# Mixing matrices of four quarters per product, contexts and mixed bias by batch, and an accumulating bias transfer in a four-layer kernel

## The chip, the cores and the metric

The kernel runs on one core of one Trainium2 chip. The core has five engines that work side by side: TensorE (PE, matmuls, with its weight loads shown as PEld), VectorE (DVE), ScalarE (ACT), GpSimd (POOL) and SyncE (SP). Here SP issues nearly all DMA transfers and POOL the rest; each of the two works through its own queue in order, and a transfer that waits for something holds up what is behind it in its queue. The metric is the time of one execution in microseconds (us) on the device. The time before is 2033.86 us, the median of three runs (2033.33 to 2036.02).

## The reference, cut to what matters

The input `x` is 32 batches of 64 rows by 1024 columns, in float32. Four layers follow one another, each of the form `x = x + ffn(cond(x))`, where `cond` mixes rows under a condition vector of 128 values per batch.

```python
# layers 0 and 3: every batch has its own 64 x 64 mixing matrix and bias
h = gelu(embedding @ W0 + b0); h = gelu(h @ W1 + b1)
att = softmax(h @ W2 + b2)                             # 32 x 8
agg_w = einsum('bk,koi->boi', att, weight[..., 0])     # 8 matrices of 64 x 64, mixed
agg_b = att @ bias_k                                   # "mixed bias", 32 x 64
out = einsum('boi,bih->boh', agg_w, x) + agg_b[:, :, None]
# layers 1 and 2: a grouped convolution over the columns
out = conv(x, weight) + (c @ c_weight.T)[:, :, None] + bias[None, :, None]   # "context"
# ffn of layer 0: top-1 routing over 8 low-rank experts
# ffn of layer 1: row-wise int8 quantization, a 1024 x 1024 product, + bias[None, :]
# ffn of layer 2: dense product + bias, and top-2 routing over 16 experts
# ffn of layer 3: squared-relu and latent products, then a layer norm
```

## The kernel before, in words

The 2048 rows are 16 tiles of 128 rows, so a tile `j` holds two batches. A tile of `x` is kept in a padded form of 8 segments of 129 columns (`W` = 1032), which makes the convolution's windows plain slices. Between the layers the tiles lie in DRAM as `xd[1]`, `xd[2]` and `xd[3]`. The program is written as straight Python loops; a planner orders the instructions of each engine and each queue by its own costs and by when buffers come free, so loads appear earlier in the SP queue than in the text.

**Start.** `condition(0)` and `attention(0, ...)` (lines 135 to 166) make `att[0]`, the attention transposed, 8 by 32. `aggregate` (lines 168 to 184) mixes the matrices: for each of four quarters `q` it loads 8 rows by 1024 values of `wk` (L174), makes two products of 32 rows by 512 (L178; each is two records in the trace), evicts one on ACT (L180) and one on DVE (L182), and stores 32 by 1024 values to DRAM (L183). `block_diagonal` (L192) loads these as `aw`, 128 by 128 per tile.

**Layer 0** (lines 399 to 434) is a software pipeline over `j`: `project` (L311, `z`), `route` (L320 with the mixed bias `bb`, L321 with `aw`), `turn`, `give` (L351 to L353, which stores `xd[1][j]` and loads it back by rows with L233 as `g`), and `conv1` (L242, L245), which adds the context `cb1`. `contexts` (lines 199 to 215) makes `cb` for all 128 partitions at once: POOL multiplies the weights by the condition for 8 batches at a time (L206, `cpr`), a product with a matrix of ones sums over the partitions (L213), and DVE adds `fside` (L214); it does so four times. For layer 1 its temporaries come from the six-buffer pool of `xT` and `w1` (`w4`). At `j` = 8 and 9 the condition of layer 3 is computed.

**Layer 1** (lines 439 to 586) begins when `cmax` of all tiles is known. In every step PE makes two products of `y` split in two parts (`hi`, `lo`, L509) and small ones for the row scales (L467, L483, `rb`), DVE does most of the quantization, and `deliver` (lines 514 to 517) multiplies on DVE into one of two buffers `t` (L516) and adds to `x` on POOL (L517). The tile then goes to `xd[2]` (L580). `x` is loaded up to five tiles ahead (`x_from`, L121), into a buffer that the store of an older tile frees, and POOL adds the bias to it (L555), in two halves. At `j` = 8, `contexts(2, ...)` makes layer 2's context.

**Layer 2** (lines 589 to 747) starts with the rows of two tiles and one convolution. Then come `aggregate(3, ...)` and, at lines 726 to 737, the mixed bias of layer 3 for all partitions, `ab3`: POOL (L729), a product with ones (L736) and a copy on ACT (L737), four times. After these the convolution of tile 1 and the steady loop follow: a logits product (L612, `lg`), 32 records of the base product (L654), transposes, 32 records of the experts' product (L664). Beside it, pieces of layer 3's weights are loaded (L686), summed on DVE and stored (`usum`, `dsum`, L695). `ab3` and layer 3's `aw` are first read in `mix` (L794, L795).

**Layer 3** (lines 750 to 1032) works in four blocks of four tiles. `second` makes seven products by the scheme of a fast matrix multiplication; `times` (lines 926 to 939) streams five weight tiles and uses each for two tiles `t`. After the last, "3", DVE adds (L775), takes statistics (L954) and `leave` normalizes (L960 to L965) and stores (L966).

Of the kernel before, what the change touches and what calls it, by code (L numbers as in the profile page):

```python
# [39 lines left out]
P = 128  # L40
# [22 lines left out]
def four_layers(ctx: ExitStack, tc: tile.TileContext, a: dict, out: bass.AP):  # L63
# [32 lines left out]
    hp = const("hp", a["hp"], (NB, P + NT + 2 * KC), nc.sync)  # L96
# [53 lines left out]
    def attention(n, h2, W2):  # L150
# [11 lines left out]
        ps = bank(f"attT_{n}", (KC, NB))  # L162
        nc.tensor.transpose(ps, ex, ident[:NB, :NB])
        atT = cst.tile([KC, NB], F32, name=f"attT_{n}")
        nc.vector.tensor_copy(atT, ps)
        return atT

    def aggregate(n, tmp_in, tmp_out):

        d = dram.tile([NB, 64, 64], F32, name=f"agg_{n}")  # L170
        flat = d.rearrange("b i o -> b (i o)")
        for q in range(4):
            w = tmp_in(f"wk_{n}_{q}")[:KC, :]
            nc.sync.dma_start(out=w, in_=a[f"wk_{n}"][:, ts(q, D)])  # L174
            t = tmp_out(f"ag_{n}_{q}")[:NB, :]
            for h in range(2):
                ps = bank(f"ag_{n}_{q}_{h}", (NB, HF))
                nc.tensor.matmul(ps, att[n], w[:, ts(h, HF)], start=True, stop=True)  # L178
                if h == 0:
                    nc.scalar.copy(t[:, ts(h, HF)], ps)  # L180
                else:
                    nc.vector.tensor_copy(t[:, ts(h, HF)], ps)  # L182
            nc.sync.dma_start(out=flat[:, ts(q, D)], in_=t)  # L183
        return d
# [14 lines left out]
    def contexts(n, pool, tmp):  # L199

        cw = small.tile([P, 64], F32, tag="ctxw", name=f"ctxw{n}")
        nc.gpsimd.dma_start(out=cw, in_=a[f"cwT_{n}"])
        cb = pool.tile([P, NB, 64], F32, name=f"cb{n}")
        for q in range(4):
            pr = tmp(f"cpr{n}_{q}").rearrange("p (b o) -> p b o", o=64)[:, 0:8, :]
            nc.gpsimd.tensor_tensor(  # L206
                pr,
                cw[:, None, :].to_broadcast([P, 8, 64]),
                condT[:, ts(q, 8), None].to_broadcast([P, 8, 64]),
                ALU.mult,  # L210
            )
            ps = bank(f"cb{n}_{q}", (P, 8, 64))
            nc.tensor.matmul(ps, ones, pr, start=True, stop=True)  # L213
            nc.vector.tensor_tensor(cb[:, ts(q, 8), :], ps, fside[:, None, :].to_broadcast([P, 8, 64]), ALU.add)  # L214
        return cb

    def mixed_bias(n, j, bk, eng):
# [4 lines left out]
            att[n][:, ts(j, 2), None].to_broadcast([KC, 2, 64]),  # L222
# [36 lines left out]
    with tc.tile_pool(name="q", bufs=1) as qp:  # L259
# [15 lines left out]
        with tc.tile_pool(name="l0", bufs=1) as lp:  # L275
# [15 lines left out]

            load(0)
# [107 lines left out]
            for j in range(NT + 6):  # L400
# [20 lines left out]
                if j == 1:  # L421
                    cb1 = contexts(1, lp, w4)
# [16 lines left out]
        with tc.tile_pool(name="w1", bufs=2) as wp:  # L439
            bias1 = small.tile([P, D], F32, tag="bias1", bufs=1, name="bias1")  # L440
            nc.gpsimd.dma_start(out=bias1, in_=a["bias1"].partition_broadcast(P))
# [95 lines left out]
            for j in range(-3, NT):  # L537
# [12 lines left out]
                if j == 8:  # L550
                    cb2 = contexts(2, k2, lambda name: wp.tile([P, HF], F32, tag="t", name=name))
                if 0 <= j + 2 < NT:
                    xs[j + 2] = x_from(f"x1_{j + 2}", xd[1][j + 2])
                    for h in range(2):
                        nc.gpsimd.tensor_tensor(  # L555
                            xh(xs[j + 2], h), xh(xs[j + 2], h), halved(bias1[:, ts(h, HF)]), ALU.add
                        )
# [32 lines left out]
    with tc.tile_pool(name="l2", bufs=1) as lp, tc.tile_pool(name="w2", bufs=7) as wp, tc.tile_pool(  # L590
# [134 lines left out]

        ab3 = c3.tile([P, NT, P], F32, name="ab3")
        for q in range(4):
            bb = w4(f"bb3_{q}")[:KC, 0:HF].rearrange("k (b o) -> k b o", o=64)
            nc.gpsimd.tensor_tensor(  # L729
                bb,  # L730
                att[3][:, ts(q, 8), None].to_broadcast([KC, 8, 64]),
                bk3[:, None, :].to_broadcast([KC, 8, 64]),
                ALU.mult,
            )
            ps = bank(f"ab3_{q}")
            nc.tensor.matmul(ps, ones[:KC, :], bb.rearrange("k b o -> k (b o)"), start=True, stop=True)  # L736
            nc.scalar.copy(ab3[:, ts(q, 4), :].rearrange("p j t -> p (j t)"), ps)  # L737
# [13 lines left out]
    with ExitStack() as l3:  # L751
# [158 lines left out]
        def second(k, between):  # L910
# [15 lines left out]
            def times(name, ps, lhs, src, go):  # L926
                for q in range(NP3 // 2):
                    w = stream(f"d_{b}_{name}_{q}", src(q))
                    for n in range(2):
                        for t in range(2):  # L930
                            i = 2 * q + n
                            nc.tensor.matmul(  # L932
                                ps[t],
                                lhs(i)[:, ts(t, P)],
                                w[:, ts(n, HF)],
                                start=(go and i == 0),
                                stop=(i == NP3 - 1),
                                skip_group_check=not go,
                            )
# [16 lines left out]
            def leave(t):  # L956
                for i in range(2):
# [45 lines left out]
            for o, p in zip(c(0, 1), p3):  # L1003
                add(o, p, o)
            finish(0, 1)
            leave(0)
# [127 lines left out]
```

## Time and profile before

| what | value |
|---|---|
| median of three runs | 2033.86 us (2033.33 to 2036.02) |
| the profiled execution's own time | 2033.69 us |
| its span, first to last instruction | 2031.9 us |
| PE busy | 1939.8 us, 95% of the span |
| DVE busy | 772.2 us, 38% |
| ACT busy | 241.8 us, 12% |
| POOL busy | 218.8 us, 11% |
| DMA moved | 316.50 MB, 156 GB/s in the mean |
| mean granted TensorE clock | 0.976 |

A group line of the profile gives the source line, the engine, the operation, the tile that is written and those that are read, shapes, how often it occurs, and behind a bar the busy time, the mean of one, and the idle time before it with what ended it. In the timeline a line is start, duration, engine, line, operation; the brackets hold the engine's idle time before it and what it waited for. In the list of waits a line has the waiter, what it waited for, and then the total in us, the number of waits and the longest. The granted clock is the share of full speed that TensorE was allowed. Matmul ends are modelled, so PE's busy time says where it was occupied rather than how well.

### The profile page before, as it was taken

Reading aid. Unit: us, or ns where it says so; the run is one execution under the profiler, and the core shown is the slowest. Engines: PE = TensorE matmul, PEld = TensorE weight load, DVE = VectorE, ACT = ScalarE, POOL = GpSimd, SP = SyncE. Lnnn points to the kernel's source line nnn. Section 1 sums busy time; section 2 is a strip of 40 time slices with the busy share of each in tenths; the row PEclk is TensorE's granted clock in tenths of the full one; section 3 lists DMA queues with packets and bytes.
Section 4 is the critical chain, followed back from the end, with each engine's and each line's share of the span. In section 5 each row is a group of like instructions: output and inputs, shape, how many; then the busy total and the mean of one; then the engine's idle time right before and its main releaser. Section 6 shows DMA issues by size and latency. Waiting matters only on the chain.

```text
span 2031.9 us, 18897 instructions
## 1 busy us (share of the span) xinstructions
PE 1939.8 (95%) x7338; PEld 1230.3 (61%) x7338; DVE 772.2 (38%) x1566; ACT 241.8 (12%) x611; POOL 218.8 (11%) x181
## 2 busy tenths in 40 slices
PE   6999897899999999999699999999999999999997
PEld 3777475645555555554488544885448864488643
DVE  3655596545541212121444224441234422353213
ACT  1221685310000000000000000000000000000000
POOL 2002055610000000000200001100001000010000
PEclk9989898979999999999799999999999999999999
DMA  7856353587950101001544544644445454454542
GB/s 229 301 189 219 112 186 132 182 255 265 320 177 32 63 32 63 11 21 43 197 156 145 167 144 166 207 157 165 145 172 196 159 167 155 155 187 147 171 150 91
DMA packets 134393, 316.50 MB, mean 156 GB/s; under 512 B 17424, under 2 KB 51248, under 8 KB 134304
## 3 DMA queue, kind: packets, MB, share of 16 engines
q1 hardware_dynamic: 133568, 313.09, 45.4%
q0 software_dynamic: 736, 2.21, 0.3%
q8 instruction: 58, 0.95, 0.2%
q14 instruction: 31, 0.25, 0.0%
HBM read 257.39 MB, written 57.87 MB: 155 GB/s over the span
## 4 chain that ended last, share of the span: by engine, by line
PE 87%; DMA 5%; DVE 3%; issue 2%; POOL 2%; ACT 1%; SPq 0%; POOLq 0%; DVEq 0%; ACTq 0%
PE d L932 24%; PE u L842 23%; PE o L664 11%; PE o L654 10%; PE conv L242 5%; PE oo L509 2%; DMA xd<-x 2%; PE z L311 2%; PE mix L794 2%; PE o L351 1%; PE lg L612 1%; PE g L525 1%; DMA x<-xd 1%; DMA wk<-in_wk_dram 1%; PE gp L801 1%
## 5 line engine op out<-in xcount | busy, mean ns | idle before, releaser
L932 PE MATMUL d<-d,h 128*128 128x512 f32 x640 | 278.8, 593 | 0.0
L664 PE MATMUL o<-bt,pT 128*128 128x512 f32 x512 | 224.0, 595 | 0.5 <-ACT pT L661 0.3
L654 PE MATMUL o<-base,yT 128*128 128x512 f32 x512 | 223.0, 593 | 0.0
L932 PE MATMUL d<-d,s 128*128 128x512 f32 x480 | 208.3, 593 | 0.0
L932 PEld LDWEIGHTS d<-d,h 128*128 128x128 f32 x640 | 120.3, 190 | 144.6 <-issue 140.9
L775 DVE TENSOR_TENSOR h<-u,h 128x256 f32<-128x256 f32 x200 | 84.8, 424 | 263.0 <-PE u L842 261.6
L664 PEld LDWEIGHTS o<-bt,pT 128*128 128x128 f32 x512 | 96.0, 190 | 118.3 <-issue 114.6
L654 PEld LDWEIGHTS o<-base,yT 128*128 128x128 f32 x512 | 96.1, 190 | 114.8 <-issue 111.0
L932 PEld LDWEIGHTS d<-d,s 128*128 128x128 f32 x480 | 90.7, 190 | 114.5 <-issue 113.3
L923 POOL TENSOR_TENSOR fin<-xf,beta 128x512 f32<-128x512 f32 x32 | 53.1, 1687 | 982.6 <-DMA out_dram<-fin 955.7
L842 PE MATMUL u<-y,uc 128*128 128x256 f32 x640 | 151.4, 379 | 0.9 <-DVE h L775 0.9
L842 PE MATMUL u<-y,ua 128*128 128x256 f32 x640 | 151.6, 379 | 0.0
L842 PE MATMUL u<-t,ub 128*128 128x256 f32 x640 | 146.9, 383 | 0.0
L242 PEld LDWEIGHTS conv<-cw,g 128*128 128x128 f32 x1024 | 123.9, 197 | 19.6 <-issue 16.6
L842 PEld LDWEIGHTS u<-t,ub 128*128 128x128 f32 x640 | 123.0, 192 | 16.9
L666 DVE TENSOR_TENSOR x<-x,o 128x512 f32<-128x512 f32 x32 | 21.9, 687 | 291.9 <-PE o L664 291.9
L842 PEld LDWEIGHTS u<-y,ua 128*128 128x128 f32 x640 | 121.4, 190 | 18.6 <-issue 2.3
L842 PEld LDWEIGHTS u<-y,uc 128*128 128x128 f32 x640 | 121.4, 190 | 18.1 <-DVE h L775 1.7
L242 PE MATMUL conv<-cw,g 128*128 128x128 f32 x1024 | 125.5, 280 | 3.4 <-DMA g<-xd 3.4
L775 DVE TENSOR_TENSOR tot<-d,tot 128x512 f32<-128x512 f32 x40 | 27.4, 686 | 197.7 <-PE d L932 197.7
L606 POOL TENSOR_TENSOR x<-x,bias 128x512 f32<-128x512 f32 x32 | 41.1, 1304 | 370.9 <-DMA x<-xd 346.7
L842 PE MATMUL u<-t,ud 128*128 128x256 f32 x320 | 75.6, 379 | 0.0
(185 smaller groups left out, 1844.9 us busy)
## 6 DMA issues: line engine op xcount, KB each, us to landing
d<-dsum SPq DMA_DIRECT2D x80, 512.0 KB, 3.4
xd<-x SPq DMA_DIRECT2D x48, 516.0 KB, 2.9
x<-xd SPq DMA_DIRECT2D x48, 516.0 KB, 4.3
d<-in_dn_dram SPq DMA_DIRECT2D x48, 512.0 KB, 3.4
ua<-in_up_dram SPq DMA_DIRECT2D x40, 512.0 KB, 4.3
ub<-usum SPq DMA_DIRECT2D x40, 512.0 KB, 4.5
uc<-usum SPq DMA_DIRECT2D x40, 512.0 KB, 3.8
g<-xd SPq DMA_DIRECT2D x32, 516.0 KB, 4.3
```

The costliest lines, as they stand in the source:

```text
L242: nc.tensor.matmul(ps[:, g, :], rows[:, 4 * b + g, ds(w, P)], cwt[:, g, w, :], start=(w == 0), stop=(w == 1))
L311: nc.tensor.matmul(ps, t[:, c, :], ra[:, c, :], start=(c == 0), stop=(c == NC - 1))
L509: nc.tensor.matmul(po, t[:, c, :], cbt[:, c, ts(n, HF)], start=(c == 0 and i == 0), stop=(c == NC - 1 and i == 1))
L606: nc.gpsimd.tensor_tensor(xh(xs[j], h), xh(xs[j], h), halved(bias2[:, ts(h, HF)]), ALU.add)
L654: nc.tensor.matmul(po[n], yT[:, c, :], base[c][:, ts(n, HF)], start=(c == 0), stop=False)
L664: nc.tensor.matmul(po[n], pT[:, c, :], bt[c][:, ts(n, HF)], start=False, stop=(c == NC - 1))
L666: nc.vector.tensor_tensor(xh(xs[j], n), xh(xs[j], n), halved(po[n]), ALU.add)
L775: nc.vector.tensor_tensor(o, p, q, op)
L794: nc.tensor.matmul(ps[:, c, :], seg(x, 4 * h + c), aw[:, j, :], start=True, stop=True)
L842: nc.tensor.matmul(ps[:, 0:TH], w[:, ts(c, P)], r[:, c, :], start=(go and c == 0), stop=(c == 3), skip_group_check=not go,)
L923: nc.gpsimd.tensor_tensor(by(fin), xh(xf, h), by(beta), ALU.add)
L932: nc.tensor.matmul(ps[t], lhs(i)[:, ts(t, P)], w[:, ts(n, HF)], start=(go and i == 0), stop=(i == NP3 - 1), skip_group_check=not go,)
```

## The change

`attention` repeats the attention four times over and masks it, so that `att[n]` is a block-diagonal matrix: 32 rows (four quarters of 8) by 4 by 32. `aggregate` then loads `wk` once, with the four quarters below one another, and makes one pair of products of 128 rows by 512; two evictions and four stores follow. The mask is in four new columns of `hp`.

A new function `by_batch` makes a product with one row per batch (32 rows), evicts it on DVE and stores it to DRAM. `contexts` becomes one load that repeats the stored row of 2048 values in all 128 partitions; both layers' contexts come from one product near the start. The mixed bias of layer 3 is made in the same way.

The bias of layer 1 is kept in DRAM in the padded form. Instead of two POOL additions per tile, POOL issues a transfer that adds it to the loaded `x` tile (`accum_op`), repeated to all partitions from one row. The load of `bias1` into SBUF goes.

In layer 3, `times` issues its five weight loads ahead of its products, and in the last block the last product is sorted so that the first tile is complete before the second begins; after "3", addition, statistics and `leave` are done tile by tile.

```diff
-        ps = bank(f"attT_{n}", (KC, NB))
-        nc.tensor.transpose(ps, ex, ident[:NB, :NB])
-        atT = cst.tile([KC, NB], F32, name=f"attT_{n}")
-        nc.vector.tensor_copy(atT, ps)
+        ex4 = small.tile([NB, 4, KC], F32, tag="ex4", name=f"ex4_{n}")
+        nc.vector.tensor_copy(ex4, ex[:, None, :].to_broadcast([NB, 4, KC]))
+        ps = bank(f"attT_{n}", (4 * KC, NB))
+        nc.tensor.transpose(ps, ex4.rearrange("b q k -> b (q k)"), ident[:NB, :NB])
+        atT = cst.tile([4 * KC, 4, NB], F32, name=f"attT_{n}")
+        nc.vector.tensor_tensor(
+            atT,
+            ps[:, None, :].to_broadcast([4 * KC, 4, NB]),
+            hp[:, ds(P + NT + 2 * KC, 4)][:, :, None].to_broadcast([4 * KC, 4, NB]),
+            ALU.mult,
+        )
...
     def aggregate(n, tmp_in, tmp_out):
+        w = tmp_in(f"wk_{n}")[: 4 * KC, :]
+        nc.sync.dma_start(out=w, in_=a[f"wk_{n}"])
+        t = tmp_out(f"ag_{n}")
+        for h in range(2):
+            ps = bank(f"ag_{n}_{h}")
+            nc.tensor.matmul(
+                ps, att[n].rearrange("k q b -> k (q b)"), w[:, ts(h, HF)], start=True, stop=True
+            )
+            if h == 0:
+                nc.scalar.copy(t[:, ts(h, HF)], ps)
+            else:
+                nc.vector.tensor_copy(t[:, ts(h, HF)], ps)
         for q in range(4):
-            w = tmp_in(f"wk_{n}_{q}")[:KC, :]
-            nc.sync.dma_start(out=w, in_=a[f"wk_{n}"][:, ts(q, D)])
-            t = tmp_out(f"ag_{n}_{q}")[:NB, :]
-            for h in range(2):
-                ps = bank(f"ag_{n}_{q}_{h}", (NB, HF))
-                nc.tensor.matmul(ps, att[n], w[:, ts(h, HF)], start=True, stop=True)
...
-            nc.sync.dma_start(out=flat[:, ts(q, D)], in_=t)
+            nc.sync.dma_start(out=flat[:, ts(q, D)], in_=t[ds(q * NB, NB), :])
...
+    def by_batch(name, lhsT, rhs, plus=None):
+        w = rhs.shape[-1]
+        ps = bank(name, (NB, w))
+        nc.tensor.matmul(ps, lhsT, rhs, start=True, stop=True)
+        t = small.tile([NB, P], F32, tag="bybatch", name=f"{name}_s")[:, :w]
+        if plus is None:
+            nc.vector.tensor_copy(t, ps)
+        else:
+            nc.vector.tensor_tensor(
+                t.rearrange("b (n o) -> b n o", o=64), ps.rearrange("b (n o) -> b n o", o=64), plus, ALU.add
+            )
+        d = [dram.tile([NB, 64], F32, name=f"{name}_d{k}") for k in range(w // 64)]
+        for k, v in enumerate(d):
+            nc.sync.dma_start(out=v, in_=t[:, ts(k, 64)])
+        return d
+
+    def contexts(n, pool):
         cb = pool.tile([P, NB, 64], F32, name=f"cb{n}")
-        for q in range(4):
-            pr = tmp(f"cpr{n}_{q}").rearrange("p (b o) -> p b o", o=64)[:, 0:8, :]
...
+        src = ctx12[n - 1].rearrange("b o -> (b o)").partition_broadcast(P)
+        nc.sync.dma_start(out=cb.rearrange("p b o -> p (b o)"), in_=src)
         return cb
...
+            cw12 = small.tile([P, 2, 64], F32, tag="row", bufs=7, name="cw12")
+            nc.sync.dma_start(out=cw12, in_=a["cwT"])
+            ctx12 = by_batch(
+                "ctx12", condT, cw12.rearrange("p n o -> p (n o)"), fside[:NB, None, :].to_broadcast([NB, 2, 64])
+            )
             load(0)
             aw = block_diagonal(0, agg0, lp)
...
-            bias1 = small.tile([P, D], F32, tag="bias1", bufs=1, name="bias1")
-            nc.gpsimd.dma_start(out=bias1, in_=a["bias1"].partition_broadcast(P))
...
                     xs[j + 2] = x_from(f"x1_{j + 2}", xd[1][j + 2])
-                    for h in range(2):
-                        nc.gpsimd.tensor_tensor(
-                            xh(xs[j + 2], h), xh(xs[j + 2], h), halved(bias1[:, ts(h, HF)]), ALU.add
-                        )
+                    nc.gpsimd.dma_start(out=xs[j + 2], in_=a["bias1"].partition_broadcast(P), accum_op=ALU.add)
...
+        (ab3d,) = by_batch("ab3", att[3][:KC, 0, :], bk3)
         ab3 = c3.tile([P, NT, P], F32, name="ab3")
-        for q in range(4):
-            bb = w4(f"bb3_{q}")[:KC, 0:HF].rearrange("k (b o) -> k b o", o=64)
...
+        nc.sync.dma_start(
+            out=ab3.rearrange("p j t -> p (j t)"), in_=ab3d.rearrange("b o -> (b o)").partition_broadcast(P)
+        )
...
             def times(name, ps, lhs, src, go):
+                ws = []
+                order = [(q, n, t) for q in range(NP3 // 2) for n in range(2) for t in range(2)]
+                if name == "3" and b == NT // 4 - 1:
+                    order.sort(key=lambda v: v[2])
                 for q in range(NP3 // 2):
                     w = stream(f"d_{b}_{name}_{q}", src(q))
...
+                    ws.append(w)
+                for q, n, t in order:
+                    i = 2 * q + n
+                    nc.tensor.matmul(
+                        ps[t],
+                        lhs(i)[:, ts(t, P)],
+                        ws[q][:, ts(n, HF)],
...
             times("3", p3, lambda i: k.s1[:, i, :], block(1, 1), False)
-            for o, p in zip(c(0, 1), p3):
-                add(o, p, o)
-            finish(0, 1)
-            leave(0)
+            for i in range(2):
+                add(c(0, 1)[i], p3[i], c(0, 1)[i])
+                nc.vector.bn_stats(st[i][:, 1, :], c(0, 1)[i])
+                leave(0, i)
```

## The prediction

> **What bounds the kernel now.** I read the busy totals, then the chain that ended last, then the waits and the timeline of the four places that the diff touches.
>
> The page first. Times are us:
>
> ```profile
> PE 1939.8 (95%) x7338; PEld 1230.3 (61%) x7338; DVE 772.2 (38%) x1566; ACT 241.8 (12%) x611; POOL 218.8 (11%) x181
> PE 87%; DMA 5%; DVE 3%; issue 2%; POOL 2%; ACT 1%; SPq 0%; POOLq 0%; DVEq 0%; ACTq 0%
> ```
>
> PE holds 87% of the chain, most of it in layers 2 and 3, whose matmuls the change leaves alone. What can move lies in the other 13% and in PE work that the diff removes. The diff touches four stretches: the start, layer 1, the start of layer 2, the last product.
>
> Start, chain in order of time (start, length, what):
>
> ```profile
> 4.72 10.20 DMA wk<-in_wk_dram
> 14.97 3.63 PE ag L178 x4
> 21.46 6.42 DMA wk<-in_wk_dram
> 27.93 3.62 PE ag L178 x4
> ```
>
> Four small loads and four products alternate. The waits of the SP queue say why a 32 KB load takes so long: it stands behind the store of the quarter before, which waits for an eviction.
>
> ```profile
> SPq L183 <- DVE ag L182: 21.9, 4, 8.3
> SPq L286 <- PE cb L213: 7.1, 1, 7.1
> ```
>
> Layer 1, timeline of the one place where PE stands still, then the chain ahead of it:
>
> ```profile
> 308.93 0.70 PE L483 MATMUL rb<-dg,ones 128*128 128x256 f32 x2 [1.21 <-ACT dg L478]
> 319.37 2.08 PE L213 MATMUL cb<-cpr,ones 128*128 128x512 f32 x2 [9.74 <-POOL cpr L206]
> 325.79 2.42 PE L509 MATMUL oo<-cbt,hi 128*128 128x512 f32 x8
> ...
> 299.05 2.85 DMA xd<-x
> 301.92 3.10 DMA x<-xd
> 305.14 3.34 POOL x L555 x2
> 308.48 1.15 POOL x L517
> ```
>
> Elsewhere the product follows `rb` by 0.35 us; here by 16.9. POOL's `cpr` is queued behind a bias add (L555), that behind a load, the load behind the store that frees its buffer.
>
> Start of layer 2, timeline:
>
> ```profile
> 404.54 7.00 PE L178 MATMUL ag<-wk,attT 8*32 8x512 f32 x8 [5.81 <-DMA wk<-in_wk_dram]
> 412.99 7.05 PE L178 MATMUL ag<-wk,attT 8*32 8x512 f32 x8 [1.45 <-DMA wk<-in_wk_dram]
> 419.96 7.19 PE L736 MATMUL ab<-bb,ones 8*128 8x512 f32 x8
> 427.08 5.83 PE L242 MATMUL conv<-cw,g 128*128 128x128 f32 x32
> ```
>
> PE goes through 22.5 us of preparation for layer 3 before the convolution that layer 2 needs.
>
> The end, timeline:
>
> ```profile
> 2020.12 0.69 DVE L775 TENSOR_TENSOR tot<-d,tot 128x512 f32<-128x512 f32 x1 [4.68 <-PE d L932]
> 2026.71 1.29 DVE L965 SCALAR_TENSOR_TENSOR fin<-tot,rs,fin 128x1024 f32<-128x1024 f32 x1
> ```
>
> After the last matmul DVE finishes two tiles in turn, 7.9 us to 2028.0, then the last store.
>
> **Part 1, the start: -15 us.** The attention gains a DVE copy and a wider last step: +0.4 us, twice (the second, in layer 0, ends a PE wait of 4.3 us at 108 to 112, so it counts: +0.4). Sixteen matmul records of 0.9 us become four (same 512 columns, 32 rows for 8): 3.6 us from 9.6, to 13.2. One eviction more, 0.69; four stores at 0.33 of SP each, to 15.2; 2.0 to land; the two `aw` loads 1.4 of SP and 5.4 to land (the row of layer 2). So `aw` is in SBUF at about 24, where its first user, `lh` at L321, started at 45.7: at most 21.7 earlier. This counts `cb` as gone from PE (4.1 us at 39.6 to 44) and the wait of `xT` for `cb` (7.1). New on SP: the `cw12` load, two 8 KB stores that wait for a product and a DVE add, and a `cb1` load that waits for one of these to land (about 2 us). Queued behind are `xT`, `w1` and `x`; DMA already queued covers it, and without cover it costs 2 to 4.
> The other limit is the supply. 13.9 MB had landed by 60 us, and the first convolution started at 61.7. q1 moved 313.09 MB in 45.4% of 2031.9 us, so 339 GB/s when all engines work. 13.9 less 0.5 for `bias1` plus 1.0 for `cb1` is 14.4 MB: 42.5 us of full use, and 46 with the first landing at 3.6. That is 15.5 earlier if all prefetches must come first, more if not. After that, layer 0 goes at PE's pace (8.6 us a step) beside a DMA share of 0.83 to 0.98, with little to give back. I take 15, ends 5 (supply) and 21.
>
> **Part 2, layer 1: -10.5 us.** The contexts' matmuls, `cpr` and four DVE adds go. The stall is 16.9 - 0.35 = 16.5, less 0.8 that the next step made up (325.79 to 333.98 against a usual 9.0): -15.7. In their place a 1 MB load on SP, which nothing near needs: 3 us of a DMA share of 0.45.
> The bias adds (L555, two by 1.2 to 1.7) become one POOL transfer of 516 KB. Issuing one costs POOL 0.5 to 0.7 (its DMA rows). It still waits for the load of `x`, with L517 queued behind it on POOL, and for L517 wait the store on SP and, through two buffers `t`, DVE at L516.
> Its own duration is shown nowhere. It moves at least what a load does, 528 KB at 339 GB/s = 1.56 us of all engines; at most I reckon three passes (source, old value, result), 4.7. I take 3.1, the middle. Sixteen of them add 50 us to the 72 (0.45 x 160) busy now in the stage.
> The loop store, load, L555, L517 came round every 10.4 us (stores at 257.41 to 309.65), slower than PE's 9.0 (`rb` at 263.12, 272.11, 281.11), and the backlog reached DVE at 299. Without L555 and with an issue it is 10.4 - 2.4 + 0.6 = 8.6; if the store shares the engines with the transfer, up to 1.56 more: 10.2. In the middle, 9.5, the backlog over 15 steps is some 7 us, about what it was when DVE first waited; I charge 5, as the last delivery (399.4, with PE's last product ended at 395.0) gates the store that SP has ahead of layer 2's first load. Hence 15.7 - 5 = 10.5. Ends: 15.7 if the loop stays under 9.0, and if 3.1 us fall wholly into the loop (11.7), 2.7 a step over 12 steps is 32 lost: +17.
> At the end of layer 0 five such transfers meet the store and load that end its chain (5.15 and 4.75 us at 179 to 189): +1.5, ends 0 and 4.7.
>
> The Trainium skill bears on this twice. Its page "DMA: Bandwidth & Descriptors", section "Issuing engines are not separate DMA queues", says that transfers started by POOL run on the same 16 engines as SP's; by it the 1.56 is charged in full, the loop is 10.2, the backlog 18 instead of 7, and the sum some 11 us worse: 2000. "SBUF — State Buffer", section "Who interferes with whom", says that a VectorE instruction with two SBUF inputs contends with GpSimd's reads; the rows agree (L503 averages 1355 ns, L488, of the same size with one operand in PSUM, 1212), and fewer POOL adds would give back 3 us of DVE.
>
> **Part 3, start of layer 2: -18 us.** 404.54 to 427.08 is 22.5. After: four `ag` records at the same 0.88, 3.5; one small product for the mixed bias, 0.3 to 0.6 by the rows of the first attention. Saved 18.4. The mixed bias then goes by store and 1 MB load to `ab3`, first read by `mix` at 982. On SP these two wait some 2 us each ahead of `g` loads, piece loads and `usum` stores; the next `g` is used after 1.9 + 13.9 us of PE work, which covers it. Without cover up to 5 us. I take 18, ends 13 and 20.
>
> **Part 4, the end: -3 us.** The last product takes 17.3 us; sorted by tile, the first half is done 8.7 earlier and its 4.8 us of DVE work and its store lie beside matmuls. The second tile needs 0.7 + 0.7 + 0.2 + 0.5 + 0.1 + 1.3 + 1.3 = 4.8 for 7.9. Ends 2.5 and 4. In the earlier blocks the DVE steps only change order: PE lost 0.9 us there in 260, cost nil. Five weight loads ahead of their products keep SP's order: nil.
>
> **Sum.** -15 + 0.4 - 10.5 + 1.5 - 18 - 3 = -44.6. The profiled execution took 2033.69, 0.17 under the median of the three: 1989.
>
> **Rivals.**
> *Slow accumulation.* The transfer lies in the loop for 3.1 us or more. For: the chain runs through this loop from 247 to 326. Against: buffers of `x` five deep. Part 2 becomes +17: 2016.
> *Front hidden.* DMA was 0.94 and 0.98 busy at 60 to 80; an earlier front waits there. Part 1 becomes -5: 1999.
> *Nothing shares.* The loop stays at 8.6, so part 2 is -15.7, part 1 -18, the tail of layer 0 free: 18 - 0.4 + 15.7 + 18 + 3 = 54, so 1979.
> *Slower.* One mechanism: the accumulating transfer in layer 1's loop. It decides where it cancels the rest: parts 1, 3, 4 and the stall give 15 - 0.4 - 1.5 + 18 + 3 + 15.7 = 50, over 12 steps 4.2 a step above 9.0, a loop of 13.2, a transfer 4.6 us in the way, the upper bound. At 6 us, 14.6: 2051.
> *Not as said.* A planner orders each queue; were stores or loads placed ahead of work that hides them, parts 1 and 3 give half: 2006.
>
> **How the numbers follow.** Forecast 0.45, nothing shares 0.15, front hidden 0.13, slow accumulation 0.12, not as said 0.08, slower 0.07. The range goes from 1970 (all four parts at their good ends, 60, and 3 for DVE work that POOL's adds no longer slow) to 2016; outside it lie slower, some of slow accumulation and a little below, about 0.15. A measurement can tell 0.2%, 4 us: faster 0.91, same 0.02, slower 0.07.
>
> **What would show it.** Part 1: one `wk` load in the chain, L321 of layer 0 starting at 24 to 31. Part 2: no PE gap over 2 us within layer 1; stores of layer 1 every 9 to 10 us; the accumulating transfers landing within 5 us of issue. Part 3: under 5 us of `ag` and mixed-bias matmuls. Part 4: one tile's DVE steps after the last matmul. I am wrong if stores of layer 1 come over 11 us apart, or if PE waits anew for `g` at 25 to 100 us.

## The result and the profile after

The changed kernel takes 2007.01 us, the median of four runs (2006.23 to 2012.54), against 2034.94 for the kernel before, again four runs (2033.33 to 2041.85). The ratio is 0.9862, with a 95% interval of 0.9833 to 0.9891. The forecast was 1989, with a range of 1970 to 2016: the direction is right, but only 27 us of the 44.6 came. The profiled execution took 2007.33, with a span of 2005.5, 26.4 shorter than before.

The page of the changed kernel, busy totals and the chain that ended last:

```profile
PE 1914.5 (95%) x7294; PEld 1232.1 (61%) x7294; DVE 773.1 (39%) x1556; ACT 235.9 (12%) x601; POOL 175.2 (9%) x150
PE 87%; DVE 5%; DMA 4%; ACT 2%; issue 1%; POOL 1%; SPq 0%; DVEq 0%; ACTq 0%; POOLq 0%
```

PE and POOL do less, as the diff says. In the chain DVE rises from 3% to 5% while its busy time stays the same (772.2 and 773.1), so PE now waits for DVE more often than before.

**Start.** First the chain in order of time (start, length, what), then a row of the PE timeline, both of the changed kernel, and the same product before:

```profile
9.44 3.79 PE ag L185 x4
13.26 0.70 DVE ag L191
...
15.33 2.23 DMA agg<-ag
...
19.06 6.19 DMA xT<-in_xT_dram
```

```profile
24.25 0.47 PE L342 MATMUL lh<-z0s,aw 128*128 128x136 f32 x2 [2.30 <-DMA aw<-agg]
```

```profile
45.70 0.40 PE L321 MATMUL lh<-z0s,aw 128*128 128x136 f32 x2
```

One product, one store, one load where four of each alternated. The first product that reads `aw` starts at 24.25 instead of 45.70, and the first convolution starts at 47.87 instead of 61.71, so 13.8 earlier.

**End of layer 0.** The fused product that opens layer 1 (`g`, L544, before L525) starts at 190.3 instead of 197.7. That is only 7.4 earlier: 6.4 of the 13.8 are lost on the way. The chain there, of the kernel before and then of the changed one:

```profile
178.73 5.15 DMA xd<-x
...
183.93 4.75 DMA g<-xd
```

```profile
157.77 6.13 DMA xd<-x
...
165.18 8.51 DMA xd<-x
174.17 7.83 DMA xd<-x
182.07 4.46 DMA g<-xd
```

The stores that took about 5 now take 6 to 8.5, and three of them lie in the chain.

**Layer 1.** From its first product to layer 3's first `ag` it took 169.3 before (235.2 to 404.5) and takes 171.5 now (227.9 to 399.4). The 16.9 us contexts stall is gone, and the layer is not shorter. The transfers of this stage (a window over layer 1), of the changed kernel and then of the kernel before; the last number is the median time to landing:

```profile
q0 software_dynamic: 1584, 5.81, 20.8%
...
xd<-x SPq DMA_DIRECT2D x15, 516.0 KB, 4.7
x<-xd SPq DMA_DIRECT2D x15, 516.0 KB, 3.8
x<-in_bias_dram POOLq DMA_DIRECT2D x11, 516.0 KB, 5.5
```

```profile
xd<-x SPq DMA_DIRECT2D x15, 516.0 KB, 2.9
x<-xd SPq DMA_DIRECT2D x15, 516.0 KB, 3.2
```

Queue q0 carries the accumulating transfers. 20.8% of 167 us over 11 transfers is 3.16 us of all 16 engines each, so the estimate of 3.1 held. But store and load land 1.8 and 0.6 later. (The run without the transfer, below, has 2.9 and 3.6 here: the store's 1.8 goes with the transfers, most of the load's 0.6 does not.) Put the loop together by the prediction's own links: before, store 2.85, load 3.10, bias adds 3.34 and delivery 1.15 made 10.4. Now 4.7 + 3.8 + 0.9 (issue on POOL) + 1.2 (one delivery add, as at 286.71) = 10.6. The stores in the trace come close: the first at 241.01 and the sixteenth at 395.79, so 10.3 apart on average, not 9.5, though single steps range from 3.3 to 15.4. A row of the waits in the stage, changed kernel and then before:

```profile
POOL x L573 <- DMA x<-xd: 60.6, 11, 8.0
```

```profile
POOL x L555 <- DMA x<-xd: 25.3, 9, 5.3
```

POOL stands 60.6 us in front of its transfer until `x` has landed (25.3 before in front of the adds), with the deliveries queued behind.

**Start of layer 2**, PE timeline of the changed kernel:

```profile
399.45 3.75 PE L185 MATMUL ag<-wk,attT 32*128 32x512 f32 x4 [5.93 <-issue]
403.12 0.42 PE L213 MATMUL ab<-bk,attT 8*32 8x64 f32 x2
403.47 5.47 PE L258 MATMUL conv<-cw,g 128*128 128x128 f32 x32
408.77 1.91 PE L628 MATMUL lg<-ar,yT 128*128 128x80 f32 x16
```

From the first `ag` to the convolution 4.0 instead of 22.5. To `lg` it is 9.3 against 28.2.

**End.** The last two rows of DVE:

```profile
1997.25 0.69 DVE L784 TENSOR_TENSOR tot<-d,tot 128x512 f32<-128x512 f32 x1 [1.94 <-PE d L945]
...
2000.34 1.29 DVE L978 SCALAR_TENSOR_TENSOR fin<-tot,rs,fin 128x1024 f32<-128x1024 f32 x1
```

One tile's steps follow the last matmul. The last 40 records of the product, of the changed kernel and then before:

```profile
1979.88 17.33 PE L945 MATMUL d<-d,s 128*128 128x512 f32 x40
```

```profile
2003.61 17.33 PE L932 MATMUL d<-d,s 128*128 128x512 f32 x40
```

The last matmul ends at 1997.21, and from there to the end of the span it is 8.3. Before, it ended at 2020.94, and it was 11.0. The DVE row at 2020.12 that the prediction shows as coming after the last matmul had started 0.8 before its end.

### The profile page after: what moved, and what is told of

It is laid out like the page before. It is cut to its first block, busy times and chain, and to the rows that moved or that the text cites. A ratio compares the mean times of both kernels' runs of the same rounds, so it can differ in the third digit from the quotient of the medians.

```text
span 2005.5 us, 18775 instructions
## 1 busy us (share of the span) xinstructions
PE 1914.5 (95%) x7294; PEld 1232.1 (61%) x7294; DVE 773.1 (39%) x1556; ACT 235.9 (12%) x601; POOL 175.2 (9%) x150
## 4 chain that ended last, share of the span: by engine, by line
PE 87%; DVE 5%; DMA 4%; ACT 2%; issue 1%; POOL 1%; SPq 0%; DVEq 0%; ACTq 0%; POOLq 0%
PE d L945 24%; PE u L851 23%; PE o L680 11%; PE o L670 11%; PE conv L258 5%; DMA xd<-x 2%; PE oo L528 2%; PE z L332 1%; PE lg L628 1%; PE g L544 1%; PE mix L803 1%; PE gp L810 1%; PE o L372 1%; DVE y L516 1%; DMA x<-xd 1%
## 5 line engine op out<-in xcount | busy, mean ns | idle before, releaser
L851 PEld LDWEIGHTS u<-t,ub 128*128 128x128 f32 x640 | 122.9, 192 | 16.9
L622 POOL TENSOR_TENSOR x<-x,bias 128x512 f32<-128x512 f32 x32 | 46.4, 1470 | 375.3 <-DMA x<-xd 228.0
L528 PE MATMUL oo<-cbt,hi 128*128 128x512 f32 x256 | 74.3, 436 | 4.3 <-ACT hi L518 4.3
```

Of the source, the lines that this page charges most:

```text
L528: nc.tensor.matmul(po, t[:, c, :], cbt[:, c, ts(n, HF)], start=(c == 0 and i == 0), stop=(c == NC - 1 and i == 1))
L622: nc.gpsimd.tensor_tensor(xh(xs[j], h), xh(xs[j], h), halved(bias2[:, ts(h, HF)]), ALU.add)
L851: nc.tensor.matmul(ps[:, 0:TH], w[:, ts(c, P)], r[:, c, :], start=(go and c == 0), stop=(c == 3), skip_group_check=not go,)
```

## The experiments

Each kernel is an edit of the changed one. Most ran once. Runs of one kernel lay up to 13 us apart (nine of the kernel before, taken beside bias_by_pe, 2028.99 to 2042.21), so smaller differences are read from stages of the trace. A stage is steadier: pool_adds_early and pool_adds_timed are the same kernel, and they differ by 3.0 in layer 1 and by 1.5 at the fused product. "Layer 1" in the table is the time from its first product to layer 3's first `ag`, "fused" is when the fused product starts. The theory at the outset: the accumulating transfer, through its traffic, eats what the stall's end gives. The rival: it is POOL's wait for `x`, with deliveries behind it.

| kernel | time | fused | layer 1 | L516, mean ns |
|---|---|---|---|---|
| before | 2033.69 | 197.7 | 169.3 | 1290 |
| changed | 2007.33 | 190.3 | 171.5 | 1955 |
| no_bias | 1980.65 | 185.3 | 150.6 | 1245 |
| wait_only | 1996.55 | 190.0 | 159.9 | 1438 |
| traffic_only | 2002.37 | 184.5 | 166.3 | 1214 |
| pool_adds | 2008.87 | 187.0 | 176.5 | 1620 |
| pool_adds_early | 2002.55 | 184.9 | 170.1 | 1398 |
| pool_adds_timed, profiled | 2005.01 | 183.4 | 173.1 | 1446 |
| part2_undone | 2003.24 | 188.6 | 170.2 | 1248 |
| contexts_after | 2012.97 | 191.6 | 177.6 | 1564 |
| contexts_pe | 1991.51 | 187.1 | 160.5 | 1281 |
| bias_by_pe, profiled | 1986.56 | 187.3 | 155.5 | 1281 |
| four_quarters | 2032.76 | 205.5 | 170.9 | 2005 |
| tail_before | 2009.46 | 192.6 | 170.7 | 2005 |

(L516 is DVE's sum of `y` and `xi`; L497 before, and another line number in some of the kernels.)

### no_bias: the transfer left out

```diff
-    nc.gpsimd.dma_start(out=xs[j + 2], in_=a["bias1"].partition_broadcast(P), accum_op=ALU.add)
```

> The accumulating transfer is taken out and nothing put in its place, so layer 1's bias is missing from the result. Both theories name this transfer as what cost layer 1 and the end of layer 0, so both expect the same. In the changed kernel fuse begins at 190.5 us, layer 1's products at 227.9, and the first mixing product of layer 3 at 399.4. Here fuse should begin at about 184 (the 6.4 us lost at the end of layer 0 come back), and from layer 1's first product to the mixing product should take about 157 us for 171.6 (16 steps of 9.0 us and what lies around them). The total: about 1988 for 2007. If it stays above 2000, the transfer is not the cause and both theories fall.

1980.65, 7 under what was expected: the bias by transfer costs 26.7, of which 20.9 in layer 1, where the stores now come 8.9 apart, and 5.0 at the end of layer 0. So the loop over `x` really was the bound of layer 1. Without the bias the step is PE's 9.0, with a wait of 0.7 left in it. One row of the windows from 150 to 190 us, the changed kernel and then this one (us, then busy times, granted clock, DMA share, GB/s):

```profile
150.00:190.00 40.00, 31.41 (x209) 27.55 (x208) 19.69 (x36) 0.71 (x3) 4.43 (x5) 0.91 0.86 236
```

```profile
150.00:190.00 40.00, 34.83 (x223) 28.39 (x222) 22.56 (x42) 2.58 (x10) 0.00 (x0) 0.96 0.56 185
```

Five transfers turn a DMA share of 0.56 into 0.86 just where layer 0's last stores and loads are in PE's way.

### wait_only and traffic_only: the transfer's two costs apart

The first keeps the transfer's place, its wait and its issue, with 128 columns in place of 1032; the second sends all the bytes, into a scratch tile, after a DVE step instead of after the load of `x`.

```diff
-    nc.gpsimd.dma_start(out=xs[j + 2], in_=a["bias1"].partition_broadcast(P), accum_op=ALU.add)
+    nc.gpsimd.dma_start(                                                    # wait_only
+        out=xs[j + 2][:, 0:128], in_=a["bias1"][0:128].partition_broadcast(P), accum_op=ALU.add
+    )
```

```diff
+    scr = k2.tile([P, W], F32, name="scr")                                  # traffic_only, once
...
-    nc.gpsimd.dma_start(out=xs[j + 2], in_=a["bias1"].partition_broadcast(P), accum_op=ALU.add)
+    nc.vector.tensor_copy(scr[:, 0:1], fresh[-1][:, 0:1] if fresh else cmax[:, 0:1])
+    nc.gpsimd.dma_start(out=scr, in_=a["bias1"].partition_broadcast(P), accum_op=ALU.add)
```

> The accumulating transfer covers 128 of 1032 columns (64 KB for 516), so most of the bias is missing from the result; POOL still waits for the same load of x before it can issue it, and the two deliveries are still queued behind it. Theory 'traffic' (the transfers take the 16 engines away from the store and the load in the loop): as good as without the bias, layer 1 about 157 us, total about 1988, stores of layer 1 land in about 3 us. Theory 'wait' (POOL stands before the transfer until x has landed, then runs its two additions back to back into VectorE's addition of y and xi, which takes 2.0 us in the mean for 1.3 before): layer 1 stays at 167 or more, total 1998 or more, that addition stays near 2.0 us.

> The same accumulating transfers go into a scratch tile that nothing reads, released by a VectorE result of the step before, so POOL does not wait for a load of x; the bias is missing from the result. They begin only after layer 0. Theory 'traffic': layer 1 stays at about 170 us with stores of 4.5 us or more; total about 2001, since only the end of layer 0 is relieved. Theory 'wait': layer 1 about 157 us, total about 1989.

Against the 150.6 of no_bias, layer 1 takes 9.3 more in wait_only. From there to the changed kernel, whose transfers differ from these by their bytes alone, it takes 11.6 more. So both theories are partly right. traffic_only takes 15.7 more than no_bias, but that is no price of the traffic alone: all sixteen transfers lie in layer 1 here, against eleven, and its one scratch tile brings a wait of its own. The DVE step writes into that tile and waits for the transfer before, and POOL waits for the DVE step:

```profile
POOL scr L577 <- DVE scr L576: 31.6, 8, 6.3
...
DVE scr L576 <- DMA scr<-in_bias_dram: 11.1, 7, 2.9
```

Neither of the two brings the DVE row to the changed kernel's 1955 ns. First the row before and in the changed kernel, then the timeline of the changed kernel and that of no_bias:

```profile
L497 DVE TENSOR_TENSOR y<-y,xi 128x1024 f32<-128x1024 f32 x16 | 20.6, 1290 | 0.0
```

```profile
L516 DVE TENSOR_TENSOR y<-y,xi 128x1024 f32<-128x1024 f32 x16 | 31.3, 1955 | 0.0
```

```profile
270.19 0.89 POOL L573 DMA_DIRECT2D x<-in_bias_dram  x1 [5.96 <-DMA x<-xd]
...
270.79 2.64 POOL L536 TENSOR_TENSOR x<-x,o 128x512 f32<-128x512 f32 x2
...
270.93 3.60 DVE L516 TENSOR_TENSOR y<-y,xi 128x1024 f32<-128x1024 f32 x1
```

```profile
265.85 1.21 DVE L516 TENSOR_TENSOR y<-y,xi 128x1024 f32<-128x1024 f32 x1
265.95 2.17 POOL L536 TENSOR_TENSOR x<-x,o 128x512 f32<-128x512 f32 x1 [4.07 <-DVE rm L493]
```

In no_bias DVE starts 0.1 before POOL, takes 1.21, and POOL's add takes 2.17, where one alone takes 1.2. In the changed kernel POOL has waited 6 us for `x`; when it is free, both halves of a delivery are due at once and start 0.14 before DVE. DVE's instruction then takes 3.60: it ends 1.1 after POOL's second add, about its own length. So it looks as if it did nothing until POOL was through. Over sixteen tiles, (1955 - 1290) x 16 is 10.6 us of DVE, and it reaches the chain: of the stage's chain this row made up 2.0% before (235 to 405 us) and makes up 10.6% now (228 to 400). What it costs layer 1 by itself is not shown, though: contexts_after, below, has the same transfers, this row at 1564, and the longest layer 1 of all. The Trainium skill, page "SBUF — State Buffer", section "Who interferes with whom", says that a VectorE instruction with two SBUF inputs contends with a GpSimd instruction that reads SBUF. That whoever issues first holds the shared ports for the whole instruction, while the other fully blocks, it says there of VectorE's 2-port modes. The rows above agree with both, for this instruction with two inputs too. The prediction drew on the same section, but only for the count of POOL adds; what changed was who starts first.

One thing is open. In wait_only, L516 accounts for 3.1 of the 9.3 and the split's second half (L522, 1295 against 1216 ns) for 1.3; the other 5 were not traced further. Nor is it clear how much of the loss at the end of layer 0 is the wait's: wait_only's fused product is as late (190.0) as the changed kernel's, but there a store issued at 151.02 took 5.93 to land, while the 16 engines were only 10% busy from 154 to 156, after a load of instruction code between 152 and 154. That this load was the cause was not tested.

### pool_adds: POOL's adds in place of the transfer

```diff
+    bias1 = k2.tile([P, D], F32, name="bias1")                              # filled after layer 0
...
-    nc.gpsimd.dma_start(out=xs[j + 2], in_=a["bias1"].partition_broadcast(P), accum_op=ALU.add)
+    for h in range(2):
+        nc.gpsimd.tensor_tensor(xh(xs[j + 2], h), xh(xs[j + 2], h), halved(bias1[:, ts(h, HF)]), ALU.add)
```

> The rest of the change stays, the accumulating transfer alone is undone: POOL adds the bias from SBUF as before, with the bias tile in the pool of layer 1's end so that it fits. Theory 'traffic': store and load are as short as before (2.9 and 3.2), fuse begins at 184, layer 1 has no stop for the contexts and takes 160 to 165 us; total 1993 to 1997. Theory 'wait': POOL still waits for x and has 2.4 us of additions more in each step, layer 1 takes 171 or more; total 2001 or more.

2008.87, as the theory of the wait expected. But here the bias tile is loaded after layer 0, so the first five tiles get their adds late, which the kernel before did not have to do. It says little about the adds themselves, so the next runs repeat it with the bias in BF16, which fits beside layer 0.

### pool_adds_early, pool_adds_timed and part2_undone: layer 1 as before

```diff
+    bias1 = small.tile([P, D], BF16, tag="bias1", bufs=1, name="bias1")     # filled in layer 0
...
-    nc.gpsimd.dma_start(out=xs[j + 2], in_=a["bias1"].partition_broadcast(P), accum_op=ALU.add)
+    for h in range(2):
+        nc.gpsimd.tensor_tensor(xh(xs[j + 2], h), xh(xs[j + 2], h), halved(bias1[:, ts(h, HF)]), ALU.add)
```

part2_undone also makes layer 2's contexts by POOL and PE, as the kernel before did.

> The change with its transfer undone: POOL adds the bias again, two adds a tile, from a BF16 tile that is there from layer 0 on, so that the first five tiles get their bias before layer 1, as in the kernel before. Theory (without the contexts' stall the loop of store, load, POOL's work and delivery binds anyway, at 10.4 a step as in the earlier run with POOL adds): products of layer 1 in 160 to 167 us, the second convolution done and the fused product started at 184 to 186, time 2003 to 2009. Rival (that earlier run was slow only because the first five tiles' adds came late): products in 145 to 152, time 1988 to 1994, and the transfer is then a loss of 13 or more against POOL's adds.

> The change with POOL's bias adds in place of the transfer (BF16 bias tile, there from layer 0 on), timed. If the transfer is a loss against the adds, as one look said (2002.6 against 2007.3): ratio to the kernel before between 0.982 and 0.986, below the 0.9862 of the change. If the two are alike: 0.986 or above.

> The change with all that it does in layer 1 undone: bias adds on POOL (from the BF16 tile) and layer 2's contexts by POOL and TensorE, as before. Theory (the loop of store, load and POOL's work bound layer 1 before, so the contexts' stall lay inside it): products of layer 1 in 159 to 161 as before, against 156.8 with the contexts loaded, so 2003 + 3 = 2006, between 2004 and 2008. Rival (the stall was 15.7 on the path): products in 170 or more, 2016 to 2020.

With the adds on POOL a single run gave 2002.55, just under the 2003 to 2009 of the theory and far from the rival; timed, the median of four runs is 2005.32 (2001.44 to 2006.68), the ratio 0.985 (0.9831 to 0.9868). Its interval overlaps that of the changed kernel, so transfer and adds can't be told apart by their times. By stages they differ at the end of layer 0 alone: layer 1 takes 170 to 173 by either, while the fused product starts at 184.9 and 183.4 with the adds and at 190.3 with the transfer.

part2_undone is the sharpest of the runs. All that the change does in layer 1 is undone, but for the BF16 bias tile, the contexts' stall is back, and the time is 2003.24, just under the 2004 that the theory allowed. Its PE timeline:

```profile
308.96 2.08 PE L247 MATMUL cb<-cpr,ones 128*128 128x512 f32 x2 [9.68 <-POOL cpr L240]
311.22 4.38 PE L247 MATMUL cb<-cpr,ones 128*128 128x512 f32 x6 [0.18 <-POOL cpr L240]
```

A gap of 9.68 and 6.5 us of matmuls, 16 in all, and yet the layer takes 170.2, against 170.1 and 173.1 with the contexts loaded. The loop over `x` needs 10.2 a step there with and without the contexts (stores from 238.15 to 391.76 and from 235.51 to 388.80, fifteen steps each), PE 9.0. So in this run PE lost in the stall what it would have waited for `x` anyway. The rival of 2016 to 2020 is out.

### contexts_after and contexts_pe: the contexts alone

Both make only layer 2's contexts as before; the second on top of bias_by_pe (next).

```diff
-    cb2 = contexts(2, k2)
+    cb2 = contexts2(2, k2, lambda name: wp.tile([P, HF], F32, tag="t", name=name))   # the old function
```

> The change, with its accumulating transfer, and only layer 2's contexts made again by POOL and TensorE. Theory (the loop binds): 0 to 5 more than the 2007.3 of the change, 2007 to 2012, with a PE gap of 5 to 17 at the contexts' matmuls that is mostly made up. Rival (their stall adds to the path): 2020 or more.

> The kernel with the bias added by TensorE, with one thing of the change undone: layer 2's contexts made again in layer 1 by POOL products and four matmuls. Theory (the stall before came from POOL's queue, which stood behind the bias adds and their wait for `x`; without these `cpr` is on time): four matmuls at about 1.04 each (2.08 for two in the row of before), so 4 more, 1990, between 1988 and 1993, and no PE gap over 3 in layer 1. Rival (the contexts themselves stall PE, whatever POOL does): 15 more, 2001 or above.

The contexts' rows, of contexts_after and of contexts_pe:

```profile
315.55 6.21 PE L247 MATMUL cb<-cpr,ones 128*128 128x512 f32 x8 [6.98 <-POOL cpr L240]
```

```profile
303.35 4.56 PE L247 MATMUL cb<-cpr,ones 128*128 128x512 f32 x6 [2.11 <-POOL cpr L240]
```

With the transfer kept, 2012.97: 5.6 over the changed kernel, slightly above what was expected. Of the 13.2 us of gap and matmuls 6.1 show in layer 1 (177.6 against 171.5), so here the loop hides only half of them; why not all, as in part2_undone, was not traced. With the bias on PE, 1991.51: 5.0 over its base in time and in layer 1, and the longest wait of PE at the contexts is 2.11. So contexts by load are worth about 5 us in these two runs, nothing that shows in part2_undone, and nowhere the 15.7 of the stall. The long gap came with the bias work in POOL's queue, adds or transfer, and its wait for `x`: without them `cpr` is nearly on time.

### bias_by_pe: the bias out of the loop

```diff
...
+    nc.vector.reciprocal(r1, scb)
+    nc.vector.tensor_tensor(bdiv, b1, r1, ALU.mult)                # bias over the scales, BF16, once
+    nc.vector.tensor_scalar(mean, ones, 1.0 / P, None, ALU.mult)
...
+    nc.tensor.matmul(po, mean, bdiv[:, ts(n, HF)], start=False, stop=True)      # in product()
-    nc.gpsimd.dma_start(out=xs[j + 2], in_=a["bias1"].partition_broadcast(P), accum_op=ALU.add)
```

> The change with layer 1's bias taken out of the accumulating transfer and out of the loop over `x`: the bias divided by the weight scales is made once in BF16 (one 512 KB load, one reciprocal and one product on DVE), and one more matmul per product of layer 1 (32 in all) adds it in PSUM. Theory (the transfer's wait and its traffic cost some 26 us, PE has no such loop): the run without any bias took 1980.7; 32 matmuls of 128x512 at the 0.27 us that one of the layer's products takes are 8.6 more, so 1989, between 1987 and 1993, with layer 1's products in about 150 us and L516 near its 1245 ns of the run without the bias. Rival (any way of adding the bias in layer 1 costs what the transfer costs, because the layer's buffers are the bound): 2000 or more, products in 160 or more.

1986.15, the median of five runs (1984.28 to 1991.27): ratio 0.9765, 0.9739 to 0.9791, below the changed kernel's whole interval. This version beats both kernels. PE timeline of layer 1 in it:

```profile
269.55 2.02 PE L535 MATMUL oo<-cbt,lo 128*128 128x512 f32 x8
272.22 0.70 PE L509 MATMUL rb<-dg,ones 128*128 128x256 f32 x2 [0.65 <-ACT dg L504]
272.56 2.21 PE L535 MATMUL oo<-cbt,hi 128*128 128x512 f32 x8
274.61 2.02 PE L535 MATMUL oo<-cbt,lo 128*128 128x512 f32 x8
276.48 0.39 PE L538 MATMUL oo<-bdiv,mean 128*128 128x512 bf16 x1
```

The steps are 9.2 long, the waits after the first under 1. The 32 extra matmuls cost layer 1 4.9 against no_bias, less than the 8.6 expected.

### four_quarters: the mixing matrices by quarters again, in parts 1 and 3

```diff
-    w = tmp_in(f"wk_{n}")[: 4 * KC, :]
-    nc.sync.dma_start(out=w, in_=a[f"wk_{n}"])
...
+    for q in range(4):
+        w = tmp_in(f"wk_{n}_{q}")[:KC, :]
+        nc.sync.dma_start(out=w, in_=a[f"wk_{n}"][:, ts(q, D)])
...
```

> The change with its first part alone undone: the mixing matrices again by four quarters with a load, two products, two evictions and a store each, in layer 0 and ahead of layer 2; contexts, mixed bias, transfer and tail as changed. Theory (the gains at the start and ahead of layer 2 come from here): the first `lh` at 36 to 44 instead of 24.3, the first convolution 8 to 14 later than 47.9, the first `ag` of layer 3 to the first `lg` 11 to 13 longer than the 9.5 of the change; all of the second and most of the first lasts, 2020 to 2033. Rival (front hidden: layer 0 gives an earlier start back to its loads): of the first part under 5 lasts at the fused product, so 2016 to 2021 in all.

2032.76, 25.4 over the changed kernel. PE timeline, the start and then the start of layer 2:

```profile
26.59 3.61 PE L179 MATMUL ag<-wk,attT 8*32 8x512 f32 x4 [2.14 <-DMA wk<-in_wk_dram]
...
40.57 0.39 PE L333 MATMUL lh<-z0s,aw 128*128 128x136 f32 x2
...
58.55 1.69 PE L249 MATMUL conv<-cw,g 128*128 128x128 f32 x13 [1.97 <-DMA g<-xd]
```

```profile
413.36 7.00 PE L179 MATMUL ag<-wk,attT 8*32 8x512 f32 x8 [6.22 <-DMA wk<-in_wk_dram]
421.95 7.15 PE L179 MATMUL ag<-wk,attT 8*32 8x512 f32 x8 [1.58 <-DMA wk<-in_wk_dram]
```

The first convolution is 10.7 later, and by the fused product the difference is 15.2 (205.5 against 190.3): nothing of an early start is given back. From the first `ag` to `lg` it is 21.6 against 9.3, 12.3 more. This one edit, two products in place of eight, is worth nearly the whole gain. The rival that the front hides it is out.

### tail_before: the last product in its old order

```diff
-    order = [(q, n, t) for q in range(NP3 // 2) for n in range(2) for t in range(2)]
-    if name == "3" and b == NT // 4 - 1:
-        order.sort(key=lambda v: v[2])
...
```

> The change with the last block's product in its old order and both last tiles finished after it. Theory: the time from the last matmul to the end goes from 8.3 back to 11.8, and the last block's products lose the 0.9 that the new order gave back: 2007.3 + 3.5 - 0.9 = 2009.9, between 2009 and 2011.5. Rival (the new order costs PE nothing, the 0.9 is noise): 2010.8; the chain's row of that product, 118.7 or 119.6, tells the two apart.

2009.46. The last 40 records of the product in this run:

```profile
1979.37 17.33 PE L941 MATMUL d<-d,s 128*128 128x512 f32 x40
```

They end at 1996.70, and from there to the end of the span it is 10.9 again. The two rows of the chain that the expectation names are there: 119.60 us with 278 records in the changed kernel, 118.74 with 276 here. But they do not say that the new order costs PE 0.9. On the PE timeline the block's last products run from 1877.46 to 1997.21 in the changed kernel and from 1876.95 to 1996.70 here, 278 records and 119.75 us in both. In the old order the first tile is complete two records before the end, DVE begins there, and the chain leaves PE at that point. So the rival's premise holds, that the order costs PE nothing; its 2010.8 is too high since it adds 3.5, of which 0.9 lies beside matmuls. The new order saves 2.6 behind the last matmul.

## Why the prediction was right or wrong

In the profiled executions: -13.8 (start) + 6.4 (end of layer 0) + 2.2 (layer 1) - 18.9 (start of layer 2) - 2.7 (end) = -26.8, against -26.4 measured. The forecast was -44.6. Of the 17.8 that is missing, 12.7 lie in layer 1 and 4.9 at the end of layer 0; the other three stages are within 1 of their terms. The time lies inside the stated range because the range reached up to the sum of a rival, not because layer 1 went as the forecast had it.

- **Part 1, the start**, -15 with +0.4 for the attention: held. 13.8 by the first convolution; undone, it costs 15.2 by the fused product. The fear that the supply of loads takes 10 of it back did not come true.
- **The end of layer 0**, +1.5 with ends of 0 and 4.7: too small. Four kernels with a transfer there start the fused product at 190.0 to 192.6, eight kernels without one at 183.4 to 188.6: 5 on average. The step took two transfers of the chain as they were in the kernel before; with the engines nearly full, three stores of 6 to 8.5 entered the chain.
- **Part 2, layer 1**, -10.5: wrong, and the step that failed. It has two terms. "The stall is 16.5 ... -15.7" took a gap on PE for time on the path. The same section said that the loop came round every 10.4 while PE needs 9.0; that loop, not the stall, set the layer's length, and in part2_undone the stall costs nothing that shows (in contexts_after, with the transfer, a stop of 13.2 costs 6.1). Then the loop was to fall to 9.5 with the adds gone. It stayed at 10.3: the store lands 1.8 later, where the bound for sharing was 1.56, the load 0.6 later, of which no_bias has 0.4 too, and the deliveries that POOL holds back collide with DVE's L516. A loop of 10.3, 1.3 over PE's 9.0, over fifteen steps is 20; taking the bias out gave 20.9.
- **Part 3, the start of layer 2**, -18: held, 18.9.
- **Part 4, the end**, -3: held, 2.7, and the new order costs PE nothing, as the forecast had it. It took all 7.9 us of DVE's old steps as lying after the last matmul; the first 0.8 lay beside it.
- **The rivals.** Slow accumulation, 2016, named the right mechanism: the transfer in the loop. Its +17 was too much: it put the transfer's whole 3.1 into the loop and came to 11.7 a step, where 10.3 was measured. "Not as said" gave 2006, which is near, but for a reason that did not occur: parts 1 and 3 did all that they say.
- **The signs.** "No PE gap over 2" failed (3.57 at 317.45), "landing within 5" failed (5.5), "stores every 9 to 10" failed by 0.3. All three are signs of part 2. Of the other parts' signs one shows faintly: PE waits anew for `g` at 25 to 100, but only 1.3 us.
- The Trainium skill's page "DMA: Bandwidth & Descriptors", section "Issuing engines are not separate DMA queues", says that all transfers run on the same 16 engines, whoever starts them. The forecast by it, 2000, was nearer than the middle that was taken; the landing time of the stores agrees with it (2.9 before and in no_bias, 4.7 with the transfers); the loads, at 3.8 against 3.6 in no_bias, hardly show it.

## What to carry to other kernels

A gap on the bounding engine is worth its length only if no slower loop runs beside it: find the round-trip time of every buffer loop in the stage (store, load, preparation, use) and compare it with the engine's step, and charge the larger. Work that must wait for a load should not stand in an in-order queue ahead of work that is already due: moved into a matmul accumulation, the same bias cost layer 1 5 us in place of 21. If a chain of small products can be folded into one by putting the parts below one another, do it first; here that alone brought 25 us.

## What the runs showed that was not expected

- An accumulating transfer of 516 KB into SBUF took 3.16 us of all 16 engines, twice the 1.56 that its bytes take at the rate of ordinary loads here, landed in 5.5, and cost POOL 0.89 to issue.
- The same DVE instruction took 1.21 or 3.60 us, as it or POOL's adds started 0.1 us earlier. The changed kernel has both cases: 1.22 at 261.97, ahead of POOL's add at 262.08, and 3.60 at 270.93.
- A 9.68 us gap on PE with 6.5 us of extra matmuls behind it left the layer's length at 170.2, within the spread of the runs without them.
